# Quantile stage of a graph kernel: rests between gathers halved and set one unit earlier, two selection networks exchanged

## The chip, the core and the metric

The kernel runs on one core of a Trainium2 chip. A core has engines that work side by side and meet through semaphores: TensorE (PE, with its weight loads as PEld), VectorE (DVE), ScalarE (ACT), GpSimd (POOL) and SyncE (SP); each takes its instructions in the order in which the program gives them to it. DMA transfers are carried out by 16 DMA engines; the indirect ones, whose row numbers come from a table, are issued by POOL. The metric is the time on the device in microseconds (us), lower being better.

## The reference

4096 nodes have 128 values each (x), and a 4096 x 4096 matrix adj says who is whose neighbour, with about 32 neighbours for each node. Two layers run one after the other.

```
# layer 0: graph attention, 8 heads
Wh  = einsum('nd,hde->hne', x, W)
att = softmax(where(adj > 0, leaky_relu(f1[:, :, None] + f2[:, None, :]), -9e15))
x   = layernorm(x + elu(elu(att @ Wh, heads concatenated) @ W1 + b1))
# layer 1: quantiles over the neighbours
rank = cumsum(adj != 0, axis=1) - 1
skip = ceil(num_nbr / 2)  (1 where num_nbr <= 5)
keep = mask & ~((rank + 1) % skip == 0)      # drops at most two of the neighbours
svals = sort(where(keep, x, big), over the neighbours)   # for each of the 128 values by itself
agg  = mean of the order statistics at 0.25, 0.5, 0.75 of n_keep
x    = (0.5 * agg + 0.5 * x) @ W.T + b + x
```

So in layer 1 each node's kept neighbours' rows are fetched, and for each of the 128 columns three order statistics of the list are wanted.

## The kernel before

**Stages.** The attention stage builds neighbour lists from adj, fetches the neighbours' rows (gathers G and Gs) and writes the new rows to a table x1_d in DRAM. Before the quantile stage all nodes are sorted by their number of neighbours, so that each of the 32 tiles of 128 nodes (one per partition) has lists of about one length. The change touches only the quantile stage, which fills the last 1650 us or so.

**Units.** A tile, or a pair of tiles of like length, is a unit (line 85). There are 19, numbered from 0 here, in this order: the single tiles 0, 1, 30, 31, the pairs (28, 29), (26, 27) and so on down to (4, 5), then the tiles 2 and 3. Unit 0 and 1 have lists of 22, unit 2 of 42, unit 3 of 62, and the pairs fall from 40 to 26. Units 7 and 8 are the pairs of length 34; units 14 and 15 are the pairs (8, 9) and (6, 7) of length 28 with the targets 6, 7, 13 and 20. The pair (10, 11) has length 28 too, but other targets and so another network, which stays.

**Gathers.** One gather (line 739) fetches one slot of a tile's list: 128 rows of 128 values, one for each partition, into the unit's buffer vals. There are three such buffers, so a unit's gathers can't begin before the unit three places earlier is through. One more gather per tile brings the nodes' own rows (xs). In all there are 1060. The finished tiles go out by 32 scatters (line 748), which the program puts between the gathers.

**Selection networks.** A unit isn't sorted in full. A network of compare-and-exchange steps brings the wanted order statistics to known slots. A step (d, both, low, high) compares slot i with slot i+d for every i in a mask; both keeps minimum and maximum, low only the minimum, high only the maximum. The table NETWORKS (line 92) holds networks by list length and wanted slots; stages_of cuts each step into pieces of at most 12 slots, counted over both tiles. The function compare (line 1838) writes a piece: ACT copies the lower slots into PSUM where both ends are kept or the piece has at least 4 slots (line 1849), then DVE takes the minimum and the maximum (line 1851), one instruction for each end. A slot is 128 values wide in each partition, so a piece of 8 slots is an instruction of 128x1024.

**Order of the work.** plan_units (line 626) works out ahead of time, with constant costs (line 616), in which order the pieces of up to two running units are done and where the gathers stand among them. It lets a clock for POOL run: 1250 ns for each gather, and where the number of gathers sent so far is a multiple of CHUNK = 20 and the unit is number 2 or later, a rest of REST ns before the next. The order it writes is what counts, since each engine works in program order. At a rest it writes a mark: a memset of one value on DVE (line 1090) and a copy of it on POOL (line 1091). The mark goes before the first piece whose planned end lies at or behind the planned time of the next gathers, or earlier if a piece needs their rows. So POOL waits at a mark until DVE has come to that piece. When a unit is through, PE sums its picked slots (line 1116), which frees the buffer, and TensorE, ACT and a scatter finish the tile.

The lines of the rests are these:

```
616 COPY, COMPARE, FETCH, LAND = (150, 107), (110, 133), 1250, 2200
617 CHUNK, REST = 20, 4000
647             rests = sent % CHUNK == 0 and u >= 2
648             if rests:
649                 clock["pool"] += REST
```

Of the kernel before, what the change touches and what calls it, by code (L numbers as in the profile page):

```python
# [85 lines left out]
for u in UNITS:  # L86
    for t in u:
# [96 lines left out]
            (4, 0xf0f0f, 0x0, 0x0),  # L184
            (8, 0xf00ff, 0x0, 0x0),
            (16, 0xffe, 0x0, 0x1),
            (8, 0x7f00, 0x8000, 0x0),
            (2, 0xc0c0c, 0x0, 0x0),
            (13, 0x2, 0x0, 0x0),
            (12, 0x70f0, 0x8000, 0x0),  # L190
            (6, 0x44cc8, 0x8000, 0x4),
            (4, 0x5070e0, 0x0, 0x10),
            (7, 0x2aaa8, 0x0, 0x0),
            (5, 0x80800, 0x1020, 0x800a),
            (1, 0x80020, 0x1004000, 0x1400),
            (2, 0x840, 0x1100000, 0x0),
            (4, 0x0, 0x100000, 0x0),
            (3, 0x0, 0x0, 0x800),
            (2, 0x0, 0x4080, 0x60000),
            (1, 0x0, 0x2080, 0x80020),  # L200
        ],
    ),
    (28, (6, 13, 20)): (
# [96 lines left out]
            (8, 0x7f807f, 0x0, 0x0),  # L300
            (16, 0x3fff, 0x4000, 0x0),
            (32, 0x3, 0x0, 0x0),
            (12, 0x7bb8, 0x0, 0x0),
            (16, 0x38000, 0x0, 0x0),
            (12, 0x380070, 0x0, 0x8),
            (8, 0x3807f00, 0x0, 0x80),
            (4, 0x38387870, 0x400000, 0x0),
            (14, 0x26664, 0x40000, 0x2),
            (9, 0x0, 0x1000000, 0x1),
            (6, 0x2266644, 0x400000, 0x20),  # L310
            (15, 0x14014, 0x1400, 0x140),
            (7, 0x0, 0x1414140, 0x141414),
            (2, 0x2424240, 0x0, 0x0),
            (5, 0x0, 0x4040, 0x0),
            (3, 0x0, 0x1008000, 0x404040),
            (1, 0x1000000, 0x10100, 0x0),
            (1, 0x0, 0x0, 0x8000),
        ],
# [295 lines left out]


COPY, COMPARE, FETCH, LAND = (150, 107), (110, 133), 1250, 2200
CHUNK, REST = 20, 4000


def slots_in(who, g):  # L620
# [5 lines left out]
def plan_units(buffers):  # L626
# [10 lines left out]
    def load():  # L637
        nonlocal loaded, sent
        u = loaded
        loaded += 1  # L640
        home[u] = free.index(min(free))
        clock["pool"] = max(clock["pool"], free[home[u]])
        free[home[u]] = 1 << 60
        events.append(("load", u))
        n = plans[u][0] + 1
        for c in range(n * len(UNITS[u])):
            rests = sent % CHUNK == 0 and u >= 2
            if rests:
                clock["pool"] += REST
            if rests or c == 0:  # L650
                parts.append((clock["pool"], rests, u, []))
            parts[-1][3].append(divmod(c, n))
            sent += 1
            clock["pool"] += FETCH
            at[(u,) + divmod(c, n)] = clock["pool"] + LAND
# [20 lines left out]
    while loaded < min(buffers, len(UNITS)):  # L676
        load()
    while running or begun < len(UNITS):
# [27 lines left out]
        if not todo[u]:  # L706
            running.remove(u)
            events.append(("sums", u))
            tails += [[count + 8, "turn", u], [count + 16, "emit", u]]
            free[home[u]] = clock["dve"] + 600 * len(UNITS[u]) * len(plans[u][1])  # L710
            if loaded < len(UNITS):
                load()
# [9 lines left out]
    for i, event in enumerate(events):  # L722
        if i in ends_at:
            u, who, g, d = event[1:5]
# [1353 lines left out]
```

## Time and profile before

| what | us |
|---|---|
| median of 3 runs (3855.74 to 3874.38) | 3856.36 |
| the profiled execution, its own time | 3852.24 |
| its span, first to last instruction | 3850.5 |
| DVE busy | 2550.5 |
| POOL busy | 2295.2 |
| ACT busy | 1203.1 |
| PE busy | 794.0 |
| compares on DVE, line 1851 | 1476.3 |
| copies for them on ACT, line 1849 | 679.7 |
| gathers of the quantile stage, line 739 (1028 of lists) | 976.7 |

Busy time is the time in which an engine had an instruction at work, over the whole span; the share of one stage can be quite another. A gather's time on POOL is that of issuing it: the rows land later. In the lines of groups the shape is partitions x elements, the number behind x is how often, then come busy us in all and mean ns of one, and behind the second bar the idle time ahead of them with what ended it. In a timeline the columns are start, length, engine, line, operation, output and inputs, shapes and count, with the idle time before it in brackets.

### The profile page before, as it was taken

What the parts mean: (1) busy time and instruction counts of PE and PEld (TensorE: products, weight loads), DVE (VectorE), ACT (ScalarE), POOL (GpSimd) and SP (SyncE); (2) the same over time, 40 slices, a digit from 0 to 9 for tenths busy, and PEclk for the clock granted to TensorE, in tenths of its full rate; (3) what the DMA queues carried; (4) which work ended last, traced back from release to release, by engine and by line L of the source; (5) the groups of instructions that cost most, each with busy time, mean ns of one, the idle gap of its engine ahead of it and who ended that gap; (6) DMA issues with size and microseconds to landing.
All of it is one profiled execution on the core that took longest, in us unless ns stands there. A gap on an engine that the chain in (4) does not pass through costs nothing. (4 is left out here: it accounts for less than half of the span.)

```text
span 3850.5 us, 17586 instructions
## 1 busy us (share of the span) xinstructions
PE 794.0 (21%) x2717; PEld 445.1 (12%) x2717; DVE 2550.5 (66%) x4934; ACT 1203.1 (31%) x1875; POOL 2295.2 (60%) x2496
## 2 busy tenths in 40 slices
PE   2012232342333423233243210000000000000111
PEld 1001111121111211111112100000000000000101
DVE  7364566364533645332121658999999999999998
ACT  3021232122311222111122223444444444444443
POOL 0545567656675766646755466666666666666632
PEclk9975665666556656566565555555555555555555
DMA  5432333232331332212211111111111111111100
GB/s 170 102 106 65 96 97 106 59 100 80 92 91 47 100 89 56 49 40 51 49 40 36 41 42 42 46 46 47 44 45 46 47 46 44 46 45 47 48 23 18
DMA packets 118649, 239.37 MB, mean 62 GB/s; under 512 B 55744, under 2 KB 72128, under 8 KB 110336
## 3 DMA queue, kind: packets, MB, share of 16 engines
q0 software_dynamic: 75392, 159.16, 16.3%
q10 hardware_dynamic: 12160, 68.49, 5.2%
q1 hardware_dynamic: 30976, 10.53, 1.4%
q14 instruction: 96, 0.79, 0.1%
q8 instruction: 25, 0.41, 0.0%
HBM read 226.82 MB, written 11.18 MB: 62 GB/s over the span
## 5 line engine op out<-in xcount | busy, mean ns | idle before, releaser
L1851 DVE TENSOR_TENSOR vals<-low,vals 128x1024 f32<-128x1024 f32 (+6 forms) x1389 | 1476.3, 1094 | 122.4 <-ACT low L1849 28.6
L739 POOL DMA_INDIRECT G<-xt_d,idx x1004 | 997.9, 994 | 628.8 <-issue 317.2
L739 POOL DMA_INDIRECT vals<-x_d,idx x1028 | 976.7, 950 | 391.7 <-issue 326.5
L1849 ACT COPY low<-vals 128x1024 f32<-128x1024 f32 (+6 forms) x771 | 679.7, 887 | 932.9 <-DVE vals L1851 608.3
L1596 ACT COPY raw<-y 32x258 f32<-32x258 f32 (+1 forms) x480 | 175.0, 365 | 893.0 <-remote 555.0
L1583 PE MATMUL y<-G,pf 128*64 128x258 f32 (+1 forms) x1072 | 246.8, 529 | 684.6 <-DVE pf L1555 279.9
L1116 PE MATMUL fin<-share,vals 128*128 128x128 f32 x294 | 70.8, 416 | 1282.4 <-DVE vals L1851 881.5
L1255 DVE MAX8 first<-sgn 128x8 f32<-128x128 bf16 x1024 | 216.8, 278 | 75.6 <-issue 45.7
L1603 DVE TENSOR_SCALAR rden<-raw 128x8 f32<-128x8 f32 x32 | 6.3, 198 | 326.4 <-ACT raw L1596 221.6
L1635 DVE TENSOR_SCALAR e<-e 128x512 f32<-128x512 f32 x64 | 27.7, 434 | 285.9 <-ACT e L1662 143.7
L1116 PEld LDWEIGHTS fin<-share,vals 128*128 128x128 f32 x294 | 63.1, 312 | 1290.1 <-DVE vals L1851 796.7
L1583 PEld LDWEIGHTS y<-G,pf 128*64 128x64 f32 (+1 forms) x1072 | 118.2, 190 | 803.8 <-issue 417.5
L1227 ACT ACTIVATE sgn<-adj_t 128x2048 bf16<-128x2048 int32 x64 | 122.0, 1906 | 156.7 <-remote 70.5
L739 POOL DMA_INDIRECT Gs<-xt_d,idx x148 | 139.8, 945 | 45.1 <-issue 44.5
L1583 PE MATMUL y<-Gs,pf 128*128 128x258 f32 (+1 forms) x364 | 147.2, 514 | 24.2 <-DVE pf L1555 18.3
L1267 DVE MAX8 rec<-first 128x8 f32<-128x256 f32 x256 | 108.8, 425 | 57.5 <-remote 34.2
L1614 PE MATMUL turned<-ident,raw 128*128 128x128 f32 x256 | 66.4, 410 | 366.9 <-DVE raw L1606 274.9
L1555 DVE TENSOR_TENSOR pf<-z,own 128x512 f32<-128x512 f32 (+2 forms) x134 | 80.9, 637 | 87.1 <-remote 42.1
L1643 PE MATMUL o<-hv,W_sb 128*128 128x512 f32 (+2 forms) x160 | 91.6, 681 | 223.8 <-DVE hv L1637 179.3
L748 POOL DMA_INDIRECT rec_d<-rec,ranks x32 | 33.6, 1050 | 143.7 <-DVE ranks L1393 129.0
L1615 ACT COPY yT<-turned 128x512 f32<-128x512 f32 x64 | 65.6, 1025 | 171.7 <-PE turned L1614 75.6
L1091 POOL COPY follow<-mark 1x1 f32<-1x1 f32 x50 | 8.9, 178 | 164.2 <-DVE mark L1090 148.8
(187 smaller groups left out, 1581.2 us busy)
## 6 DMA issues: line engine op xcount, KB each, us to landing
adj_t<-in_adj_dram ACTq DMA_DIRECT2D x64, 1024.0 KB
vals<-x_d,idx POOLq DMA_INDIRECT x1028
G<-xt_d,idx POOLq DMA_INDIRECT x1004
R<-rec_d SPq DMA_DIRECT2D x128, 26.4 KB
score<-rec_d SPq DMA_DIRECT2D x184, 1.0 KB
Gs<-xt_d,idx POOLq DMA_INDIRECT x148
xt_d<-rec SPq DMA_DIRECT2D x4, 548.0 KB
rec<-in_x_dram SPq DMA_DIRECT2D x4, 512.0 KB
```

The lines of the kernel that those rows point to most:

```text
L739: nc.gpsimd.indirect_dma_start(out=dst, out_offset=None, in_=rows, in_offset=bass.IndirectOffsetOnAxis(ap=idx, axis=0),)
L1116: nc.tensor.matmul(fin[:, i, :], lhsT=v, rhs=w, start=(a == 0), stop=(a == len(terms) - 1), skip_group_check=True,)
L1227: nc.scalar.activation(sgn, adj_t, AF.Sign, accum_out=cnt[:, i : i + 1])
L1255: nc.vector.max(first[:, ts(c0 // CW + c, 8)], key[:, b * (512 // CW) + c, :])
L1267: nc.vector.max(top, first)
L1555: nc.vector.tensor_tensor(pf.rearrange("p (g k h) -> p g k h", g=g2, k=k)[:, a:], z[:, half * g2 + a - g0 : (half + 1) * g2 - g0, :].unsqu ...
L1583: nc.tensor.matmul(yv[p0 : p0 + m], lhsT=pf, rhs=rhs, start=not any(over[:i]), stop=not any(over[i + 1 :]), skip_group_check=True,)
L1596: nc.scalar.copy(raw[p0 : p0 + m, 4 * half + b - 1 : 4 * half + b + 1, :], y[p0 : p0 + m, :, a : a + D + 1],)
L1614: nc.tensor.transpose(t_ps[:, b, :], yn[:, 4 * half + b, :], ident)
L1643: nc.tensor.matmul(o, lhsT=consts["W1_sb"][:, h, :], rhs=hv[:, ts(j, n)], start=(h == 0), stop=(h == H - 1),)
L1849: nc.scalar.copy(kept, low)
L1851: nc.vector.tensor_tensor(high if end else low, kept, high, ALU.max if end else ALU.min)
```

## The change

Two things are changed. In plan_units the rest is 2000 ns in place of 4000, and rests begin with unit 1 and not with unit 2. Two networks of the table are replaced by others with the same targets: the one of length 28 for the slots 6, 7, 13 and 20, and the one of length 34. The constants of cost, the number of buffers, and all that is outside the quantile stage stay.

```diff
@@ network (28, (6, 7, 13, 20))
+            (2, 0xc0c0c, 0x0, 0x0),
             (8, 0x7f00, 0x8000, 0x0),
-            (2, 0xc0c0c, 0x0, 0x0),
             (13, 0x2, 0x0, 0x0),
             (12, 0x70f0, 0x8000, 0x0),
-            (6, 0x44cc8, 0x8000, 0x4),
-            (4, 0x5070e0, 0x0, 0x10),
-            (7, 0x2aaa8, 0x0, 0x0),
-            (5, 0x80800, 0x1020, 0x800a),
-            (1, 0x80020, 0x1004000, 0x1400),
-            (2, 0x840, 0x1100000, 0x0),
-            (4, 0x0, 0x100000, 0x0),
-            (3, 0x0, 0x0, 0x800),
-            (2, 0x0, 0x4080, 0x60000),
-            (1, 0x0, 0x2080, 0x80020),
+            (6, 0xc4cc8, 0x8000, 0x0),
+            (7, 0xaaaa8, 0x0, 0x0),
+            (4, 0xa0e0, 0x0, 0x0),
+            (1, 0x85020, 0x0, 0x402),
+            (4, 0x0, 0x500000, 0x1010),
+            (1, 0x0, 0x12000, 0x80004),
+            (5, 0x0, 0x102000, 0x20008),
+            (2, 0x840, 0x100080, 0x0),
+            (5, 0x0, 0x0, 0x8800),
+            (3, 0x0, 0x2080, 0x0),
+            (1, 0x0, 0x80, 0x20),
@@ network (34, (8, 16, 24, 25))
-            (12, 0x7bb8, 0x0, 0x0),
-            (16, 0x38000, 0x0, 0x0),
-            (12, 0x380070, 0x0, 0x8),
-            (8, 0x3807f00, 0x0, 0x80),
-            (4, 0x38387870, 0x400000, 0x0),
+            (12, 0x387848, 0x0, 0x0),
+            (8, 0x7c00, 0x0, 0x0),
+            (8, 0x38003b0, 0x0, 0x0),
+            (4, 0x38383870, 0x0, 0x8),
+            (4, 0x3c300, 0x400000, 0x80),
...
-            (5, 0x0, 0x4040, 0x0),
-            (3, 0x0, 0x1008000, 0x404040),
+            (3, 0x0, 0x1018100, 0x404040),
@@ rests
-CHUNK, REST = 20, 4000
+CHUNK, REST = 20, 2000
...
-            rests = sent % CHUNK == 0 and u >= 2
+            rests = sent % CHUNK == 0 and u >= 1
```

## The prediction

> **What bounds the kernel now.** I first cut the span into stages and asked for each engine's busy time in each. Columns: start and end, length, then busy us (count) of PE, PEld, DVE, ACT and POOL, granted clock, DMA share, GB/s.
>
> ```profile
> 2182.00:2282.00 100.00, 7.61 (x32) 6.66 (x32) 60.34 (x86) 30.86 (x54) 62.23 (x67) 0.52 0.16 44
> 2282.00:2407.00 125.00, 6.17 (x21) 4.79 (x21) 92.31 (x107) 42.13 (x60) 78.40 (x87) 0.50 0.16 43
> 2407.00:2507.00 100.00, 3.85 (x14) 3.04 (x14) 97.89 (x85) 45.95 (x52) 68.09 (x76) 0.50 0.17 46
> 3040.00:3500.00 460.00, 41.29 (x156) 34.76 (x156) 443.55 (x466) 217.10 (x278) 303.90 (x332) 0.51 0.17 45
> ```
>
> The quantile stage runs from about 2182 to 3840. From 2407 on VectorE (DVE) is busy 96 to 98% of the time: it is the bound, and the gathers on POOL lie beside it. Before 2407 it is busy only 152.6 of 225 us: the loading of the first units still shows. The chain of waits says only that the last stores end the run, so it doesn't help. Next, who waits for what in that stage (total us, times, longest):
>
> ```profile
> POOL follow L1091 <- DVE mark L1090: 148.8, 35, 15.9
> POOL vals L739 <- PE fin L1116: 46.6, 1, 46.6
> ...
> DVE vals L1851 <- DMA vals<-x_d,idx: 13.4, 1, 13.4
> ```
>
> POOL spends 149 us at rests; DVE waits openly for rows only once after its start, for 13.4 us. Last, the widths of the compares (busy, mean ns of one), which give the price of a network:
>
> ```profile
> L1851 DVE TENSOR_TENSOR vals<-low,vals 128x1024 f32<-128x1024 f32 x449 | 539.0, 1220 | 19.6 <-ACT low L1849 6.6 <-issue 4.4
> ...
> L1851 DVE TENSOR_TENSOR vals<-vals 128x256 f32<-128x256 f32 x152 | 60.5, 417 | 3.6 <-remote 2.3 <-DVE vals L1851 1.0
> ```
>
> From these two: (1220-417)/6 = 134 ns per slot of 128 values, and 417-2x134 = 150 ns per instruction.
>
> **The networks.** I split the old and new masks into pieces as stages_of does and counted. Length 34 (two units): 105 instructions on 668 slots become 106 on 660: +0.15-1.07 = -0.92 us each. Length 28 with targets (6, 7, 13, 20) (two units): 76 instructions stay, 506 slots become 500: -0.80 us each. Sum on DVE: **-3.4 us**, on the path. ACT's copies go from 53 to 52 and from 38 to 40 per unit; ACT is busy under half of the stage, so they lie under the compares. The 28 network has one more stage (20 against 19), but the next unit's pieces fill between stages. Without that cover, two units pay one hand-over through ACT each, some 2 us together (gaps of 0.3 to 0.9 us before compares that waited for a copy, doubled).
>
> **One more rest.** Rests stood before gathers 60, 80, ... 1040: 50. Now one stands before gather 40 too: 51. Each costs DVE a memset of 59 ns and POOL 0.18 us plus up to 0.5 us of start-up. The planner would put that rest before the compare that starts at 2209; POOL reaches gather 40 only at 2214, so it finds the mark set and doesn't rest, in effect. It delays the last rows of the second unit by 0.3 to 0.6 us, for which DVE waits (compare at 2221.9): **+0.5 us**.
>
> **Half the rest.** The planner's arithmetic (taken for the order it writes, not for time) makes 20 gathers 25 us, and a rest of 4 makes a cycle of 29; now 27. In the trace a gather starts every 1.25 us, and the 21 rests between 2437 and 3024 waited 70 us in all, 3.4 each: cycles of 29. So I expect POOL's waits at rests to fall to about 1.4 us each while rests pace it.
>
> Where does the freed POOL time go? POOL gets ahead until no buffer is free. How far it may: unit 5's first gather starts at 2511.8, its buffer's last compare was at 2406.8, so 105 us of lead; for unit 6 it is 96, unit 7 68, unit 8 23, and from unit 9 on 4 to 25, about what sums and order leave. Two us per 20 gathers from gather 40 on take 41 us off by unit 8 (gather 456): there the lead is gone. So **rests pace POOL for 18 cycles** (gathers 80 to 440); afterwards it waits for buffers, in lumps between units, and the wait for PE's sums grows in place of those at rests. Queued behind a waiting POOL are only later gathers and the scatters of finished tiles, for which nobody waits until the end.
>
> What DVE gains: at 2281.8 it sits 13.4 us, because the rest before gather 80 follows unit 1's last compare. That rest's due time moves from 108 to 106, ahead of the last two compares (planned ends 106.45 and 107.62), or six if the later rows shift them: those began at 2281.0 and 2279.6. **-0.8 to -2.3 us, taken -1.2.** After 2407 DVE waited for rows at no place, so earlier gathers gain nothing there.
>
> What DVE may lose. There are two stretches in which DVE stalls between compares with no data missing: 2247 to 2275 and 2373 to 2397. This is DVE in the second (start, us, ..., idle before it), with the rests of POOL at its two sides:
>
> ```profile
> 2371.95 0.41 DVE L1851 TENSOR_TENSOR vals<-low,vals 128x256 f32<-128x256 f32 x1
> 2373.78 0.42 DVE L1851 TENSOR_TENSOR vals<-low,vals 128x256 f32<-128x256 f32 x1 [1.42 <-issue]
> 2374.12 2.12 DVE L1851 TENSOR_TENSOR vals<-vals 128x256 f32<-128x256 f32 x6
> 2377.28 0.42 DVE L1851 TENSOR_TENSOR vals<-vals 128x256 f32<-128x256 f32 x1 [1.04 <-DVE vals L1851]
> 2377.68 1.49 DVE L1851 TENSOR_TENSOR vals<-low,vals 128x1280 f32<-128x1280 f32 x1
> 2385.68 2.28 DVE L1851 TENSOR_TENSOR vals<-low,vals 128x1280 f32<-128x1280 f32 x3 [6.51 <-remote]
> ...
> 2390.58 1.09 DVE L1851 TENSOR_TENSOR vals<-vals 128x256 f32<-128x256 f32 x3 [2.29 <-remote]
> ```
>
> ```profile
> 2365.67 0.18 POOL L1091 COPY follow<-mark 1x1 f32<-1x1 f32 x1 [1.48 <-DVE vals L1851]
> 2406.94 0.18 POOL L1091 COPY follow<-mark 1x1 f32<-1x1 f32 x1 [15.90 <-DVE mark L1090]
> ```
>
> The compare at 2385.68 takes the maximum of the very slots whose minimum had just run: it waits only for DVE's own count of finished instructions, which arrives late. The stalls add to 17 us in the first stretch and 14 in the second (1.42+1.04+6.51+2.29+3.10). Between 2407 and 3800 there is none like them. What sets the two apart is the density of indirect DMAs, counted as starts in the POOL timeline: the 90 us up to any point of the first stretch hold 66 to 70, up to the second 67 or 68; any other 90 us of the stage hold at most 66, but for 67 at 3650. The new cycle gives 90/27x20 = 66.7 gathers and about 2 scatters: 68 to 69. The change moves POOL to the pace at which DVE stalled. The margin is two DMAs in 90 us, so this is an inference.
>
> Its price: such a stall also holds the next mark back, and POOL then rests longer (15.9 us after the second stretch), so DVE must fall behind by what POOL sends too fast. Bounds: nothing if density isn't the cause; upper, the two stretches' own 31.9 us over 18 cycles' worth of time (225 us against 18x27 = 486), so 69 us. Between them: a harmless 90 us held 64 to 67, so 20 gathers with their 0.6 scatters need 27.7 to 29.0 us; 27 is short by 0.7 to 2.0 per cycle, times 18, 13 to 36. I take **+20**, nearer to the densest pace that is known to be harmless, and for the eleven units that load after gather 440, each in bursts at the dense pace and then a pause for a buffer, +1 each, **+11** (0 to 14 each by the second stretch).
>
> A rule of the Trainium skill speaks for no loss: "SBUF — State Buffer", section "SBUF: two separate sides", says that a DMA cannot be slowed by compute nor the reverse, contention being left to the port that GpSimd shares with Vector. By it the price is nothing and the sum -4. The trace has the port's part (a gather took up to 1.14 us in place of 0.94 while DVE worked on two SBUF inputs at 2166 to 2183), too small to matter; but the stalls stand in it with dense gathers, so I go by the row. [...]Dense increments alone would have struck every unit's tail of narrow compares; the trace has them smooth at 2502 to 2523.
>
> **Sum.** -3.4 +0.5 -1.2 +20 +11 = +27 us. The profiled execution took 3852.24 us, 1.7 over its span of 3850.5 and 4.1 under the median of the runs, 3856.36. So 3879 in that execution's terms, **3883** as a median.
>
> **Rivals.**
> - *Nothing but the networks* (0.30): the freed time turns into waits for buffers. For it: POOL waits 149 us at rests and 47 for sums as it is, and 40 gathers ran without a rest at 2526 to 2576 unharmed. 3856.4-4.1 = 3852; 3843 to 3858.
> - *Faster* (0.17): the rest before gather 40 thins the first 90 us to 66 or less, and the first stretch doesn't happen: -17.5 with the -4.1 makes 3835; without the second too, 3820. It decides at one gather or two in 90 us; against it, POOL reaches that rest late.
> - *Stalls in every unit* (0.06): the bound of 69 us above, 3921 and over.
> - That the rest isn't shortened can't be: waits at marks follow the planned due times to 1 or 2 us.
>
> **Numbers.** The stalls have 0.47, with 3860 to 3912 as their own range. A measurement here tells 0.5% from no change, 19 us: below 3837, above 3875.6. Faster: most of the third case, 0.15, and a little of the second, 0.16. Slower: 0.7 of the stalls and the last case, 0.39. Same: 0.45. The range: half of the faster case lies below 3832 and a few of the stalls above 3912: 3832 to 3912.
>
> **What would show it.** 51 copies of the mark; waits at marks of about 70 us in all in place of 149, those for PE's sums larger. More than two stretches of DVE stalls without missing rows, before 2900, each with 67 or more indirect DMAs in the 90 us ahead. If DVE stays at 97% there and its idle time between 2182 and the end stays at the 126 us that the gaps of its timeline sum to now, the density is not the cause and the second case holds; if DVE is idle under 20 us between 2182 and 2282, the third does. Compares should sum to 3.4 us less.

## The result, and the profile after

The changed kernel took **3903.44 us** in the median of 4 runs (3896.19 to 3917.82), the kernel before 3856.05 (3838.43 to 3874.38): a ratio of 1.0122, 95% interval 1.0080 to 1.0163. It is slower by 47 us. (Ratios leave out runs that lie more than 1.5% above the quickest of their kernel, which concerns experiment g2 alone.) The profiled execution took 3917.82, with a span of 3916.0. Of the 65.5 us between the two spans, 14.5 lie ahead of the first gather of the quantile stage (2162.5 before, 2177.0 after), in code that did not change; the quantile stage itself went from 1687.9 to 1739.0, **+51 us**, and that is what has to be explained.

The stages of the profile after, cut 14.5 us later than those of before. Columns as before: start and end, length, busy us (count) of PE, PEld, DVE, ACT and POOL, granted clock, DMA share, GB/s.

```profile
2196.50:2296.50 100.00, 8.17 (x32) 7.12 (x32) 59.75 (x85) 29.98 (x53) 63.20 (x70) 0.52 0.16 44
2296.50:2421.50 125.00, 5.21 (x18) 4.13 (x18) 93.17 (x109) 43.04 (x61) 83.44 (x92) 0.50 0.17 45
2421.50:2521.50 100.00, 4.81 (x16) 3.70 (x16) 97.94 (x86) 45.78 (x52) 72.13 (x79) 0.50 0.19 50
2521.50:2721.50 200.00, 13.56 (x60) 11.98 (x60) 167.19 (x180) 79.44 (x100) 122.90 (x136) 0.52 0.16 42
3054.50:3514.50 460.00, 42.90 (x156) 35.54 (x156) 429.50 (x447) 211.23 (x270) 287.82 (x314) 0.50 0.16 43
```

The first three rows are those of before to within a microsecond of DVE. The loss is in the last two: DVE is busy 429.50 us of 460 where it was busy 443.55, and 167.19 of 200 us in the stretch behind 2521.5. That stretch of the kernel before, not shown so far:

```profile
2507.00:2707.00 200.00, 16.33 (x72) 14.08 (x72) 191.68 (x200) 91.25 (x116) 131.39 (x145) 0.53 0.17 45
```

DVE did 24 us less work in the same time, and POOL 8 us less: the engine that was to get ahead issued fewer instructions (136 against 145). The clock granted to PE is the same to within 0.01. DVE does not work slower either: its compares took as long as before. The wide group before, then the wide and the narrow group after (busy us, mean ns, idle time ahead):

```profile
L1851 DVE TENSOR_TENSOR vals<-low,vals 128x1024 f32<-128x1024 f32 (+6 forms) x1389 | 1476.3, 1094 | 122.4 <-ACT low L1849 28.6 <-DMA vals<-x_d,idx 24.8 <-issue 23.7
```

```profile
L1851 DVE TENSOR_TENSOR vals<-low,vals 128x1024 f32<-128x1024 f32 (+6 forms) x1393 | 1475.0, 1089 | 177.4 <-remote 41.9 <-issue 34.5 <-ACT low L1849 32.5
L1851 DVE TENSOR_TENSOR vals<-vals 128x256 f32<-128x256 f32 (+2 forms) x189 | 72.1, 408 | 2.1 <-remote 1.8
```

In the wide group 1476.3 us were busy before and 122.4 idle ahead of them; now it is 1475.0 and 177.4. (The narrow group was busy 72.9 us before.) So the loss is 55 us of idle time between compares. Who waited for whom after, from 2200 on (total us, times, longest):

```profile
POOL follow L1091 <- DVE mark L1090: 112.6, 24, 16.2
POOL vals L739 <- DVE vals L1851: 61.2, 2, 54.2
DVE vals L1851 <- remote: 43.7, 15, 6.5
POOL vals L739 <- PE fin L1116: 43.3, 3, 23.3
DVE vals L1851 <- issue: 34.5, 55, 2.0
...
DVE vals L1851 <- DMA vals<-x_d,idx: 25.1, 3, 11.4
```

POOL waits for the marks of DVE less often (24 times in place of 35) but by no means half as long; all idle time ahead of the marks, whatever ended it, went from 164.2 to 142.2 us. What grew on DVE is waits for "remote" and "issue", which are no engine's work and no missing rows. Its waits for rows did not grow: the 25.1 us stand against 24.8 in the line of the kernel before. (They take in the first wait of the stage, 11.4 us in both kernels, which lay ahead of 2200 before.) What the new waits look like is DVE after, from 2667:

```profile
2667.16 7.39 DVE L1851 TENSOR_TENSOR vals<-low,vals 128x1024 f32<-128x1024 f32 x8
...
2674.60 0.69 DVE L1851 TENSOR_TENSOR vals<-low,vals 128x512 f32<-128x512 f32 x1
2675.92 0.69 DVE L1851 TENSOR_TENSOR vals<-low,vals 128x512 f32<-128x512 f32 x1 [0.62 <-issue]
2678.50 0.43 DVE L1851 TENSOR_TENSOR vals<-low,vals 128x256 f32<-128x256 f32 x1 [1.89 <-ACT low L1849]
2679.52 0.42 DVE L1851 TENSOR_TENSOR vals<-low,vals 128x256 f32<-128x256 f32 x1 [0.59 <-DVE vals L1851]
...
2689.45 6.22 DVE L1851 TENSOR_TENSOR vals<-low,vals 128x1536 f32<-128x1536 f32 x6 [2.02 <-ACT low L1849]
...
2699.21 1.29 DVE L1851 TENSOR_TENSOR vals<-low,vals 128x512 f32<-128x512 f32 x2 [2.61 <-remote]
2701.87 3.36 DVE L1851 TENSOR_TENSOR vals<-low,vals 128x1280 f32<-128x1280 f32 x3 [1.37 <-issue]
...
2708.87 3.61 DVE L1851 TENSOR_TENSOR vals<-low,vals 128x1280 f32<-128x1280 f32 x3 [2.34 <-ACT low L1849]
```

Up to 2675 the compares follow one another; then come gaps of 0.6 to 2.6 us for 33 us, the picture that the kernel before had in two places only. POOL's marks after, over an earlier part of the stage with two stretches of such gaps (the number in brackets is the wait):

```profile
2322.23 0.18 POOL L1091 COPY follow<-mark 1x1 f32<-1x1 f32 x1
2347.29 0.18 POOL L1091 COPY follow<-mark 1x1 f32<-1x1 f32 x1
2373.70 0.18 POOL L1091 COPY follow<-mark 1x1 f32<-1x1 f32 x1
2414.27 0.18 POOL L1091 COPY follow<-mark 1x1 f32<-1x1 f32 x1 [15.27 <-DVE mark L1090]
2442.02 0.18 POOL L1091 COPY follow<-mark 1x1 f32<-1x1 f32 x1 [2.35 <-DVE mark L1090]
2467.43 0.18 POOL L1091 COPY follow<-mark 1x1 f32<-1x1 f32 x1
2496.25 0.18 POOL L1091 COPY follow<-mark 1x1 f32<-1x1 f32 x1 [2.31 <-DVE mark L1090]
2522.44 0.18 POOL L1091 COPY follow<-mark 1x1 f32<-1x1 f32 x1 [0.48 <-issue]
2565.75 0.18 POOL L1091 COPY follow<-mark 1x1 f32<-1x1 f32 x1 [15.15 <-DVE mark L1090]
```

The three marks without a wait are followed by a stall of DVE (2386 to 2408), which the kernel before has too, and the stall by a wait of 15.27 us at the next mark; then come short waits, a stall that is new (2531 to 2556), and a wait of 15.15. A stall of DVE holds POOL back at the next mark.

**Late counts.** DVE tells the others, and itself, through a count that an instruction is done. The trace records when each count arrived. Mostly that is 0.01 us after the end of the instruction; in the gaps above it is far more, in rows of counts 1.4 us apart. I call a count that is more than 0.2 us behind its instruction late, and a run of three or more with under 12 us between them a stretch. The kernel before had 20 late counts in the quantile stage, in two stretches (2249 to 2273, 2377 to 2396). (Two or three late counts at the very end of a run, which every run has, are left out.) The changed kernel had **82, in eight**: 2261 to 2283, 2386 to 2408, 2531 to 2556, 2675 to 2708, 2945 to 2956, 3048 to 3055, 3434 to 3454 and 3613 to 3641. DVE's idle time, summed by the gaps of its timeline, rose from 126.0 to 179.5 us. These +53.5, with the 2 us off that the compares take less here (1549.2 to 1547.1), are the +51. The trace doesn't hold all counts (1020 of some 1626 in the stage after, 1049 of 1621 before), so there may be more late ones; the idle time is the firmer measure.

### The profile page after: what moved, and what is told of

It reads as the page before. It is cut to its first block, busy times and chain, and to the rows that moved or that the text cites. A ratio compares the mean times of both kernels' runs of the same rounds, so it can differ in the third digit from the quotient of the medians.

```text
span 3916.0 us, 17582 instructions
## 1 busy us (share of the span) xinstructions
PE 814.3 (21%) x2714; PEld 453.9 (12%) x2717; DVE 2548.0 (65%) x4937; ACT 1204.3 (31%) x1877; POOL 2297.7 (59%) x2497
## 5 line engine op out<-in xcount | busy, mean ns | idle before, releaser
L1851 DVE TENSOR_TENSOR vals<-low,vals 128x1024 f32<-128x1024 f32 (+6 forms) x1393 | 1475.0, 1089 | 177.4 <-remote 41.9
L1654 PE MATMUL key<-yT,W_sb 128*128 128x512 f32 (+2 forms) x160 | 99.1, 741 | 7.9 <-ACT yT L1615 5.5
```

Of the source, the lines that this page charges most:

```text
L1654: nc.tensor.matmul(hT[:, ts(j, n)], lhsT=consts["W_sb"][:, h, :], rhs=yT[:, h, 0:n], start=True, stop=True,)
L1851: nc.vector.tensor_tensor(high if end else low, kept, high, ALU.max if end else ALU.min)
```

## The experiments

The question was whether the density of the gathers makes the counts late, or something else in the new order (which compares and gathers meet), or the networks, and what the time would be without it. The runs of the experiments fell on four chips, and on one of them the kernel before takes 3465 us and not 3836 to 3856; runs are compared with the kernel before on the same chip alone. An overview first. DVE idle and late counts are those of the quantile stage in the profiled execution; the last column says for how many of the 1092 indirect DMAs of the stage the 90 us ahead held 67 or more. The profiled execution need not be a middling one: that of g1 is the second quickest of 20 (3852.91), those of g2 and g6 are the slowest of theirs (3865.18 and 3897.31).

| run | kernel before | this | ratio (95% interval) | DVE idle | late | dense |
|---|---|---|---|---|---|---|
| before | 3856.05 | | | 126.0 | 20 | 36 |
| after | 3856.05 | 3903.44 | 1.0122 (1.0080 to 1.0163) | 179.5 | 82 | 125 |
| e1: networks alone | 3464.60 | 3460.81 | 0.9987 (0.9981 to 0.9994) | 89.6 | 0 | 97 |
| e2: rests alone | 3464.60 | 3460.49 | 0.9985 (0.9977 to 0.9992) | 86.5 | 0 | 510 |
| e3: networks, rests of 4000 from unit 1 | 3464.60 | 3458.86 | 0.9985 (0.9978 to 0.9992) | 87.9 | 0 | 97 |
| e4: after, and a fill at each mark | 3464.60 | 3469.16 | 1.0014 (1.0007 to 1.0021) | 97.5 | 0 | 429 |
| f1: after again | 3836.09 | 3888.02 | 1.0142 (1.0111 to 1.0173) | 173.9 | 77 | 169 |
| f2: as e4 | 3836.09 | 3880.02 | 1.0126 (1.0091 to 1.0162) | 171.8 | 66 | 119 |
| f3: before, without marks | 3836.09 | 3950.60 | 1.0300 (1.0269 to 1.0330) | 235.9 | 123 | 141 |
| f4: as e3 | 3836.09 | 3834.71 | 0.9997 (0.9976 to 1.0019) | 123.4 | 19 | 31 |
| g1: after, and a longer fill | 3855.42 | 3867.26 | 1.0040 (1.0015 to 1.0065) | 144.4 | 19 | 9 |
| g2: 10 gathers, rests of 2000 | 3855.42 | 3845.33 | 0.9936 (0.9898 to 0.9974) | 115.1 | 30 | 16 |
| g5: as g2, from the first unit | 3840.28 | 3829.66 | 0.9966 (0.9949 to 0.9984) | 118.2 | 28 | 30 |
| g6: 10 gathers, rests of 1000 | 3840.28 | 3872.76 | 1.0082 (1.0051 to 1.0113) | 166.4 | 67 | 74 |

### The parts of the change, one at a time

Networks alone (e1), from the changed kernel:

```diff
-CHUNK, REST = 20, 2000
+CHUNK, REST = 20, 4000
-            rests = sent % CHUNK == 0 and u >= 1
+            rests = sent % CHUNK == 0 and u >= 2
```

> The kernel before with the two exchanged networks alone; rests of 4000 from unit 2 on, as before. Density theory (DVE's own count arrives late when POOL issues 67 or more indirect DMAs in 90 us): 3.4 us faster than before, about 3853; no stretches of stalls besides the two before 2400. Rival of the networks (their tails of short compares are what stalls): 20 us or more slower, with stalls while units 7, 8, 14 and 15 are at work.

Rests alone (e2), from the kernel before:

```diff
-CHUNK, REST = 20, 4000
+CHUNK, REST = 20, 2000
-            rests = sent % CHUNK == 0 and u >= 2
+            rests = sent % CHUNK == 0 and u >= 1
```

> The kernel before with the rests alone: 2000 ns, from unit 1 on; old networks. Density theory: the whole loss stays, 47 + 3 = 50 us slower than before, about 3906, with eight or more stretches of stalls. Rival of the networks: within 10 us of before.

The networks and the earlier start, with rests as long as before (e3), from the changed kernel:

```diff
-CHUNK, REST = 20, 2000
+CHUNK, REST = 20, 4000
```

> The changed kernel with rests of 4000 again, but still from unit 1 on: the one rest more, and the networks. Density theory: POOL comes to that rest late, so nothing thins before 2247, and the time is that of the networks alone, about 3853. If the first rest does harm of its own: 3865 or more. If it removes the first stretch, as the faster rival of the prediction had it: 3835.

Measured, on the chip where the kernel before takes 3464.60: 3460.81, 3460.49 and 3458.86. The networks give 3.8 us, and that can be read from the groups of the two runs, e1 first (new networks), then e2 (old):

```profile
L1851 DVE TENSOR_TENSOR vals<-low,vals 128x1024 f32<-128x1024 f32 (+6 forms) x1393 | 1473.5, 1089 | 89.4 <-ACT low L1849 37.2 <-DMA vals<-x_d,idx 26.5 <-PE fin L1116 0.3
L1851 DVE TENSOR_TENSOR vals<-vals 128x256 f32<-128x256 f32 (+2 forms) x189 | 71.9, 408 | 0.2
```

```profile
L1851 DVE TENSOR_TENSOR vals<-low,vals 128x1024 f32<-128x1024 f32 (+6 forms) x1389 | 1476.4, 1094 | 86.3 <-ACT low L1849 37.0 <-DMA vals<-x_d,idx 23.4 <-issue 0.3
L1851 DVE TENSOR_TENSOR vals<-vals 128x256 f32<-128x256 f32 (+2 forms) x191 | 73.0, 408 | 0.3
```

1545.4 us of compares against 1549.4: 4.0 less. The surprise is e2: the shorter rests, which were to cost, gave 4 us. That trace has no late count at all, although its gathers are denser than those of any other run here (510 DMAs with 67 or more in the 90 us ahead, up to 72). DVE waited for "remote" at no place of its stage. Two windows of e2 show what the changed rests do to a chip on which counts come in time (they lie as far behind the first gather as the last two of after):

```profile
2159.00:2359.00 200.00, 11.65 (x42) 9.57 (x42) 193.91 (x177) 94.12 (x111) 143.82 (x159) 0.51 0.18 49
2692.00:3152.00 460.00, 41.45 (x156) 34.80 (x156) 443.48 (x471) 215.88 (x279) 300.11 (x328) 0.51 0.17 45
```

DVE is busy 193.91 and 443.48 us, where the changed kernel has 167.19 and 429.50. So density by itself is not sufficient: the chip must be one on which counts come late. The next runs fell on such chips.

### The changed kernel again, and its rests put back to 4000

The changed kernel unaltered on a second chip (f1):

> The changed kernel itself, once more. In the first four experiments the kernel before took 3465 us and not 3856, and no trace of them has DVE waiting for a late count of its own, in whatever stage and at up to 70 indirect DMAs in 90 us. So late counts belong to the chip or its condition, and density only matters where they occur. Theory of density plus condition: where before takes about 3465, the changed kernel is within 8 us of it, rather faster (networks 3.4 us); where before takes about 3856, it is some 47 us slower. Theory of density alone: 40 us or more slower everywhere.

Measured: 3888.02, ratio 1.0142, with 77 late counts in eight stretches, at the same places of the stage, counted from its first gather, to within 9 us. The loss belongs to the kernel on such a chip and is no accident of one profile.

The same edit as e3, on this chip (f4):

> The changed kernel with rests of 4000 from unit 1 on. Where before takes about 3465: 5 us faster than before, as measured. Where it takes about 3856: density theory says 3 to 8 us faster, 35 us or more if the first stretch of stalls doesn't happen.

Measured: 3834.71, ratio 0.9997 (0.9976 to 1.0019); 19 late counts in two stretches, the two of the kernel before. Only the length of the rests differs from f1, so **the halved rest is the whole loss**, and of the chips seen here it is a loss only on those where counts come late. Its two windows stand where those of before do:

```profile
2489.00:2689.00 200.00, 16.10 (x72) 13.85 (x72) 191.55 (x200) 91.06 (x115) 131.50 (x145) 0.53 0.18 45
3022.00:3482.00 460.00, 42.29 (x156) 35.36 (x156) 444.47 (x469) 217.68 (x278) 308.67 (x338) 0.51 0.18 46
```

### No rests at all

The order of the kernel before, with nothing written at a mark (f3):

```diff
             elif kind == "mark":
-                mark = fp.tile([1, 1], F32, name="mark", bufs=4)
-                nc.vector.memset(mark, 0.0)
-                nc.gpsimd.tensor_copy(follow, mark)
+                pass
```

> The kernel before, its order and networks untouched, without the 50 marks: POOL never rests, and waits only for buffers. Where before takes about 3465: within 5 us of it, since DVE misses no rows and its counts are not late. Where it takes about 3856: density theory says slower than the changed kernel, by 60 us or more against before; if rests are worth nothing, within 5 us of before.

Measured: 3950.60, ratio 1.0300, 123 late counts in twelve stretches. The dose and the effect go together: rests of 4000, 2000 and none give 19 to 20, 77 to 82 and 123 late counts, and about 0, 47 to 52 and 115 us. What DVE waited for in this run (total us, times, longest):

```profile
DVE vals L1849 <- remote: 73.3, 27, 7.2
DVE vals L1849 <- issue: 55.0, 67, 3.1
...
DVE vals L1849 <- DVE vals L1849: 27.5, 32, 1.5
DVE vals L1849 <- DMA vals<-x_d,idx: 24.7, 3, 11.3
```

Waits for rows are as in the changed kernel (25.1 there); what grew is the kind without a worker. Here the order of all the work is that of the kernel before, so the order can't be what stalls.

### The new order at the old pace: a fill on POOL

If density is the cause, the changed order must be harmless when a batch of gathers takes longer for another reason. A fill of 2048 elements behind each mark's copy (e4, f2), added to the changed kernel:

```diff
+        pause = late.tile([1, 2048], F32, name="pause")
...
                 nc.gpsimd.tensor_copy(follow, mark)
+                nc.gpsimd.memset(pause, 0.0)
```

> The changed kernel, with its order of pieces and marks untouched, but at each of the 51 marks POOL does a memset of 2048 elements in one partition behind the mark's copy: about 2.0 us each by the trace's rows (128 elements 204 ns, 32 elements 116 ns). Density theory: the cycles of 27 us become 29, the stretches of stalls after 2450 go, idle time of DVE in the stage falls from 180 to about 126 us, and the time to about 3855. Rival of the order (the pieces in the order written for rests of 2000 stall by themselves): stays at 3903 or above, stalls where they were.

> The changed kernel with POOL's memset of 2.0 us behind each mark, order untouched, as before. Where before takes about 3465: 3 to 6 us slower than before, as measured (3469.2 against 3464.6). Where it takes about 3856: density theory says the stalls after 2450 go and the time is within 12 us of before; the rival of the order says 47 us slower.

Measured: 3469.16 where counts come in time (1.0014), and 3880.02 where they don't (1.0126): the second is a miss, since it was to come near the kernel before. The fill was too short. It took 1.79 us, and most of it only filled time that POOL would have waited at the mark: waits at marks fell from 142 us in the changed kernel to 81, and the fills took 91.5, so 30 us were added over the whole stage, and the density stayed (119 DMAs with 67 or more). The run tells nothing apart. With 3500 elements (g1) the fill took 3.0 us:

```diff
+        pause = late.tile([1, 3500], F32, name="pause")
```

> The changed kernel's order, with a fill of 1x3500 elements on GpSimd behind each mark's copy (about 3 us by the 1.79 us that 1x2048 took), so that a batch of 20 gathers comes about every 29 to 30 us instead of about 26.5, without a mark's wait on VectorE: about 46 more fills, all of them where the mark's wait stood before. Where the kernel before takes about 3,840 to 3,856: if the density of the gathers makes the stalls, the stretches after 2,450 go and the time is within 15 us of the kernel before (ratio at most 1.004); if the new order itself (what meets what) makes them, it stays at the +47 to +50 of the changed kernel (ratio 1.010 or more). Where the kernel before takes about 3,465: no late counts in either, ratio 1.000 to 1.003, and nothing told apart.

Measured: 3867.26, ratio 1.0040 (1.0015 to 1.0065), 12 us over the kernel before and at the edge of what density was to give; 19 late counts in place of some 80. A cycle of 20 gathers came every 28.1 us in the median between gather 80 and gather 440. One stretch behind 2450 was left, at 2499 to 2525. Late counts and stretches are those of a quick run, 14 us under the median. The order by itself doesn't make the loss of the changed kernel. The 12 us are no fair price of the order either: a fixed fill also holds POOL back where it is late (39.0 us of waits for rows on DVE, 25.1 in the changed kernel). How they divide was not tested.

### The pause in smaller pieces

The cleanest test of density changes only the constants of the changed kernel. Rests of 2000 behind every 10 gathers (g2) have the mean density of 20 and 4000; rests of 1000 behind every 10 (g6) that of the changed kernel. The pieces are the same.

```diff
-CHUNK, REST = 20, 2000
+CHUNK, REST = 10, 2000
```

> The changed kernel with rests of the same 2,000 planned ns behind every 10 gathers instead of 20, from the second unit on: the mean density of 20 gathers with 4,000, in shorter pieces. Where the kernel before takes about 3,840 to 3,856: if the mean density over some 90 us decides, it is like the kernel before (ratio 0.997 to 1.004, about 20 late counts); if the length of a pause decides (a queue has to run dry), it is like the changed kernel (1.010 to 1.015, 60 late counts or more). Where the kernel before takes about 3,465: 0.998 to 1.001 by both.

```diff
-CHUNK, REST = 20, 2000
+CHUNK, REST = 10, 1000
```

> The changed kernel with rests of 1,000 planned ns behind every 10 gathers: the mean density of the changed kernel (100 ns for each gather), in the shorter pieces of the run before. Where the kernel before takes about 3,840 to 3,856: if the mean density decides, it is slow like the changed kernel (ratio 1.008 to 1.015, 60 late counts or more); if shorter pieces are what helped, it is at most 1.003. Where the kernel before takes about 3,465: 0.998 to 1.001 by both.

Measured: 0.9936 (0.9898 to 0.9974) and 1.0082 (1.0051 to 1.0113), with 30 and 67 late counts. The ratio of g2 leaves out five of its twelve runs, because one at 3792.63 is so quick; over all twelve the mean is 0.996 of the kernel before. At equal pieces, the rest per gather decides: g6 is slow, if somewhat less than the changed kernel, and g2 is not slow; nor is g5 below, which was measured on the same chip as g6. DVE in the stretch of 200 us, 344.5 us behind the first gather, in g2 and in g6:

```profile
2533.70:2733.70 200.00, 18.02 (x72) 15.66 (x72) 193.74 (x203) 95.50 (x118) 132.59 (x151) 0.51 0.16 45
```

```profile
2514.00:2714.00 200.00, 17.97 (x72) 15.62 (x72) 181.34 (x197) 87.75 (x110) 136.76 (x156) 0.51 0.17 46
```

g2 was if anything faster than the kernel before, so the next run has rests in the first units as well (g5), where the kernels shown so far send 40 to 60 gathers in a row:

```diff
-CHUNK, REST = 20, 2000
+CHUNK, REST = 10, 2000
-            rests = sent % CHUNK == 0 and u >= 1
+            rests = sent and sent % CHUNK == 0
```

> The changed kernel with rests of 2,000 behind every 10 gathers from the first unit on, also inside the first 60 gathers, which no kernel so far has spread. Where the kernel before takes about 3,840 to 3,856: if density makes the first stretch too (2,268 to 2,287, 11 late counts in the run of 10 gathers), that stretch goes and the time is 5 to 10 us below that run: ratio 0.990 to 0.995 against the kernel before. The rival: VectorE waits for the first units' gathers, which now land up to 10 us later, and nothing is won: 0.994 to 1.000. Where the kernel before takes about 3,465: no stretch to take away, 0.998 to 1.003.

Measured: 3829.66, ratio 0.9966 (0.9949 to 0.9984). Faster than both kernels, by 0.3% against the one before, but not by the reason given: the first stretch is still there (2245 to 2258, 10 late counts), so the rival of that expectation holds, and the rests of the first units gain nothing to be seen. Whether and why smaller pieces are better than rests of 20 and 4000 (f4: 0.9997) was not tested by itself; they were measured against the kernel before on different chips, and not on the chip of 3465.

## Why the prediction was right, and where it was not

It said 3883, a loss of 27 us through dense gathers, with a range to 3912; it was 3903, a loss of 47 through dense gathers. The mechanism was right, for the kind of chip whose trace it had read. By its steps:

- **The networks, -3.4.** Right: 3.8 us in the time of e1, 4.0 in the compares of e1 against e2, 2.1 in those of the changed kernel against the one before. ACT's copies went from 771 to 773, as counted, and stayed hidden.
- **One more rest, +0.5.** Right in the trace: there are 51 marks, the one before gather 40 waited for nothing, and the compares behind the second unit's last rows began 59.8 us after the first gather in place of 59.4. Its worth in time isn't settled: e3 against e1, which differ in this rest alone, gives -2.0, within their intervals.
- **The wait of 13.4 us, -1.2.** On the chip without late counts it is 11.6 us in e2 and 13.5 in e1: -1.9, inside the bounds. In the changed kernel it is 10.1, but the first stretch of stalls lies ahead of it and took another course than before, so that -3.3 is not the rest's alone.
- **Waits at marks of 1.4 us.** Right for undisturbed cycles, wrong for the sum. Of the 19 marks from gather 80 to gather 440, fifteen waited 19.0 us together, 1.3 each. The other four stand behind stretches and waited 16.8, 15.3, 15.2 and 10.4. So all waits at marks are 142 us and not about 70; in e2, where nothing stalls, they are 77.9.
- **"Rests pace POOL for 18 cycles", then buffers.** Right in its place. The first gather of unit 8 (gather 456) came 23.2 us after the last compare on its buffer before; now it came 5.1 us after it, behind a wait for PE's sums that the kernel before has not:

```profile
2862.59 0.95 POOL L739 DMA_INDIRECT vals<-x_d,idx  x1 [19.48 <-PE fin L1116]
```

In e2 the two numbers are 4.9 and 18.6. The stalls took nothing of POOL's lead, since a mark holds POOL back together with DVE: from gather 80 to gather 440 it took 527.2 us, against 532.9 before, where 18 cycles shorter by 2 us would have made 36 less (484.1 in e2, against 517.9 in e1).
- **Later units at +1 each.** This is the term that was mis-sized. Behind gather 440 POOL did wait longer for buffers: the first gathers of units 8 to 18 waited 68.2 us together before, 141.5 now. But marks went on pacing it too (65.6 us of waits, 80.8 before), and the gathers between were dense enough: the last four of the eight stretches lie there. The idle time of DVE, summed over the part of the stage in which POOL sent the gathers named (the first wait for rows, 11.4 us in both, left out):

| gathers | before | after | difference | predicted |
|---|---|---|---|---|
| 0 to 240 | 63.8 | 63.1 | -1 | |
| 240 to 440 | 11.1 | 33.9 | +23 | |
| 0 to 440 together | 74.9 | 97.0 | +22 | +19 (stalls +20, rests +0.5 - 1.2) |
| from 440 on | 39.8 | 71.1 | +31 | +11 |

- **The size of the stalls.** Up to gather 440 it was nearly met, +22 against +19, in part by luck: the first eight of the 18 cycles added nothing to what the kernel before loses there, and the other ten all of the +23. Behind gather 440 the measured +31 is 2.8 us for each of the eleven units where 1 was taken, inside the bounds given for it (0 to 14). These 20 us are most of the gap between forecast and result.
- **67 DMAs in 90 us as the mark of danger.** Too sharp. The 90 us ahead of the last six stretches held 66, 65, 62, 61, 65 and 66, and e2 went to 72 unharmed. In the trace of before, too, the number held only for the greater part of the two stretches: at their ends it is 62 or 63. See the last section.
- **The rule of separate sides** ("SBUF — State Buffer" of the Trainium skill, section "SBUF: two separate sides"), by which the sum was -4. The compares bear it out: they took no longer beside denser gathers (1475.0 us in the wide group, 1476.3 before), and on the chip of 3465 the change of rests cost nothing (e2: -4 us). What doesn't follow from it is that dense gathers have no price: on the other chips they cost some 50 us, through counts. So going by the row was right there, and the row said nothing of the other kind of chip.
- **The rivals.** "Nothing but the networks" fits the chip of 3465, as far as e1 and e2 show; the changed kernel by itself was not run there. "Faster, because the first stretch goes" happened nowhere among the chips with late counts. "Stalls in every unit" lay at 3921 and over; without any marks (f3) the loss was 115 us, so that bound, 69 us, was not the end of it either.

What stays open is why the counts come late. The runs show what spaces the gathers and what follows from it, not what the count waits for.

## What to carry to other kernels

A pause that keeps a queue engine slow may be what keeps another engine fast; before it is shortened, ask whether anything waits for the time that it frees. Here DVE was the bound at 97% and nobody waited for rows, so the half rest had nothing to win, and 47 us to lose. And where a stall holds up the engine that caused it as well, the two keep their distance: count with a cycle that repeats to the end of the stage, not with a danger that passes once the lead is used up.

## What the runs showed of the hardware

- **Two kinds of chip.** The same kernel took 3464.60 us on one chip and 3836.09 to 3856.05 on the others, with a granted clock of 0.598 on the one and 0.593 to 0.594 on those of the other experiments. Of the 393 us between the profiled spans of before and e1, 352 lie ahead of the quantile stage; there before has 160 late counts of DVE and e1 none. A gain or loss of 1% found on one kind (after: 1.0122) may be absent on the other (e2: 0.9985). Only one chip was of the faster kind, and whether it is the chip or its condition at the time was not told apart.
- **A pace of 1.4 us.** A count that rises by one with each indirect DMA and falls by one every P us separates DMAs inside stretches from those outside best at P = 1.42 us (right in some 92 of 100 pairs over the ten traces with late counts; the number in 90 us is right in 82 to 90, by where a stretch is taken to begin). The fit to three of the slow kernels alone gives 1.44, that to five of the others 1.42. The late counts come 1.4 us apart, too. 20 gathers and 0.6 scatters would then need 29 us (20.6 x 1.42): the cycle that rests of 4000 make (28.65 us in the median from gather 80 to gather 440 before, 27.9 in the changed kernel). This was read from the traces afterwards, and is a description, not a cause.
- **Neither the transfers nor ACT are late.** In before, after and e2 alike a gather's last completion was written 2.2 us after POOL began it, and of the ACT counts in the changed kernel's trace 3 of 508 were over 0.2 us late. It is DVE's counts, beside dense indirect DMAs on such a chip, that are held up.
